# A graph attention layer on one core: the second layer of two steps' radial MLP as four 64x64 quadrants, and transfers spread over the steps

## The chip, the cores and the metric

The kernel runs on one core of a Trainium2 chip. The time is device time of one execution in microseconds (us); three executions of the kernel before took 6774.2, 6771.05 and 6747.99 us, median 6771.05. PE is the matmul engine (PEld its weight loads), ACT the engine for activations, DVE the vector engine, POOL the engine that issues the gathers, SP the one that issues the other transfers. Everything is float32.

## The reference

There are 12500 nodes and 400000 edges, sorted by destination. Each edge has 32 attributes, a weight, a source and a destination. Cut to what matters:

```
h       = relu(layernorm(x))
message = (h @ w_src + b_src)[src] + (h @ w_dst)[dst]
r       = silu(edge_attr @ w1 + b1)          # 32 -> 64
r       = silu(r @ w2 + b2)                  # 64 -> 64
message = message * edge_weight * (r @ w3 + b3)   # 64 -> 128
message = message @ w_sep + b_sep            # per head: 16 for the score, 16 values
score   = sum(smooth_leaky_relu(a) * alpha_dot)   # 8 heads
att     = softmax of score over the edges of one destination
out     = x + segment_sum(values * att) @ w_proj + b_proj
```

The three products with w1, w2 and w3 are the radial MLP, "first", "second" and "third layer" below.

## The kernel before

Node tables (h @ w_src, h @ w_dst) are made first. Then the edges are worked through in 400 *pairs*, numbered k; a pair is 1000 edges, two sections f = 0, 1 of 500 edges, each section four tiles of 125. At the end partial sums at the sections' ends are combined and projected. Nearly all the time is the loop over k in `passes` (from L882 on). One pass of it, a step, does the message of pair k and the weighted sums of pair c = k - 12, because the softmax needs the scores of whole groups of eight pairs.

The order on each engine is the order in which the program is written, `tc.manual_schedule()`. In step k, before the change:

- SP: the stores of pair c - 1 (win, and half of agg), then loads: every eighth step, at k % 8 = 1, the edge attributes of eight pairs (`load_e`, eight transfers of 125 KB in 128-byte rows, L688), in odd steps the destinations of two pairs (`load_d`, L695), then the weights of pair k + 2 spread over all partitions (`load_w`, 500 KB, L701) and two windows of the destination table (`load_md`, L707), and last the other half of agg (L878).
- POOL: eight gathers of source rows for pair k + 4 (L714). Their buffer gs has four copies, so the gathers of k + 4 start when the transposes of pair k (L766) have read theirs.
- PE, in this order: third layer of pair k (L754); eight transposes of gathered rows into pm (L766) and the destination rows added (L771); values of pair c, first half (L855); alphas(k, 0) (L779); values, second half; first layer of pair k + 2 (L732); second layer of pair k + 1 (L740); alphas(k, 1); sums of pair c (L866); the transposes of the attributes of pair k + 3 (`e_T`, L724); in odd steps scores (L790).
- ACT: the SiLU passes after alphas (sl, L781), first layer (h, L735) and second layer (h, L742), copies of the sums (ob, L870) and of the transposed attributes (eT, L726).
- DVE: rad = (third layer + b3) * weight (L757), mT = pm * rad (L775), pvx = values * attention (L857), al (L783) and one-hot matrices.

A product result lies in one of eight banks. Before the change these are: m1 (one bank: e_T and the second layer), p3 (two: first and third layer), pm (two), pa, misc (sums, scores, softmax transposes) and V, one each. A product that writes a bank waits until the last result there has been read. In the profile, names lose their numbers: p stands for p1 and p3, m for m1, h for h1 and h2.

The first layer packs two sections' attributes by 32 and 64 rows, so its result holds f = 0 in partitions 0 to 63 and f = 1 in 64 to 127. The second layer before is one product with a block matrix that has w2 twice on its diagonal (L740). The third layer is two products with 64 rows, one for each section (L754).

Buffers named below: `sp` and `lp` tiles have two copies unless `bufs=` says otherwise; w_b and md have three.

Of the kernel before, what the change touches and what calls it, by code (L numbers as in the profile page):

```python
# [21 lines left out]
F32 = mybir.dt.float32  # L22
BF16 = mybir.dt.bfloat16
I32 = mybir.dt.int32
AF = mybir.ActivationFunctionType
# [5 lines left out]
P = 128  # L31
C = 128
H = 8
RAD = 32
BANK = 512
FC = 64
# [9 lines left out]
T = 125  # L46
TS = 4
SEC = T * TS
W = 64
PR = 2 * SEC  # L50
# [3 lines left out]
EP = 8  # L54
# [3 lines left out]
def gnn_kernel(ctx: ExitStack, tc: tile.TileContext, a: dict, out: bass.AP):  # L58
    nc = tc.nc
# [39 lines left out]
    def load(name, shape, ap=None, eng=None):  # L99
# [14 lines left out]
    part = const.tile([P, 1], F32, name="part")  # L114
    nc.gpsimd.iota(part, pattern=[[0, 1]], base=0, channel_multiplier=1,
                   allow_small_or_imprecise_dtypes=True)
    zc = 5
    assert N % RP == 0 and N // RP % zc == 0
    z = const.tile([RP, zc * ROW], F32, name="z")
    nc.gpsimd.memset(z, 0.0)  # L120
# [482 lines left out]
    def windows():  # L603
        with tc.tile_pool(name="wk", bufs=1) as kp:
            w1b = kp.tile([P, P], F32, name="w1b")
            nc.vector.memset(w1b, 0.0)
            w2b = kp.tile([P, P], F32, name="w2b")
            nc.vector.memset(w2b, 0.0)
            w3b = kp.tile([P, C], F32, name="w3b")
            b12 = kp.tile([P, 2], F32, name="b12")  # L610
            for f in range(2):
                for q in range(2):
                    r = (2 * q + f) * RAD
                    nc.sync.dma_start(out=w1b[r:r + RAD, f * FC:(f + 1) * FC], in_=a["fc_w1"])
                s = slice(f * FC, (f + 1) * FC)
                nc.sync.dma_start(out=w2b[s, s], in_=a["fc_w2"])
                nc.sync.dma_start(out=w3b[s, :], in_=a["fc_w3"])
                nc.sync.dma_start(out=b12[s, 0:1], in_=a["fc_b1"])
                nc.sync.dma_start(out=b12[s, 1:2], in_=a["fc_b2"])
            w_s = kp.tile([C, 32], F32, name="w_s")  # L620
            nc.vector.memset(w_s, 0.0)
            nc.vector.tensor_copy(w_s[:, 0:H], w_score[:, 0:C:C // H])
            b_s = kp.tile([P, 1], F32, name="b_s")
            tgt = kp.tile([P, NP], F32, name="tgt")
            with tc.tile_pool(name="tg", bufs=1) as gp, tc.tile_pool(name="tg_ps", bufs=1, space=PSUM) as gq:
                pb = gq.tile([P, 1], F32, name="pb")
                for j in range(4):
                    nc.tensor.matmul(pb[32 * j:32 * j + 32, :], w_s, b_a, start=True, stop=True)
                nc.vector.tensor_scalar(b_s, pb, 0.25, None, op0=ALU.mult)
                tb = gp.tile([P, NP], I32, name="tb")  # L630
                nc.sync.dma_start(out=tb[0:W, :], in_=base_d[0:1, :].to_broadcast([W, NP]))
                nc.sync.dma_start(out=tb[W:P, :], in_=base_d[1:2, :].to_broadcast([W, NP]))
                row = gp.tile([P, 1], F32, name="row")
                nc.vector.tensor_copy(row, part)
                nc.vector.tensor_scalar(row[W:P, :], part[W:P, :], float(W), None, op0=ALU.subtract)
                nc.vector.tensor_scalar(tgt, tb, row, None, op0=ALU.add)
            passes(kp, w1b, w2b, w3b, b12, w_s, b_s, tgt)
        combine()

    def passes(kp, w1b, w2b, w3b, b12, w_s, b_s, tgt):  # L640
        src_t = src.rearrange("(t p) -> t p", p=T)
        dst_t = dst.rearrange("(t p) -> t p", p=T)
        ea_t = ea.rearrange("(t p) c -> p t c", p=T)
        dst_p = dst.rearrange("(k f e) -> f k e", f=2, e=SEC)
        ew_p = ew.rearrange("(k e) o -> o k e", e=PR)
        with tc.tile_pool(name="ld", bufs=2) as lp, tc.tile_pool(name="wk2", bufs=2) as sp, \
# [33 lines left out]
                nc.vector.tensor_copy(loc, pt[:, 1, :])  # L680
                prep[u] = (idx, loc)

            def load_e(g):
                e_g[g] = lp.tile([T, EP * 8, RAD], F32, name="e_t")
                for f in range(2):
                    for t in range(TS):
                        o = t % 2 * 4 + t // 2 * 2 + f
                        nc.sync.dma_start(  # L688
                            out=e_g[g][:, o::8, :],
                            in_=ea_t[:, g * 8 * EP + f * TS + t:(g + 1) * 8 * EP:8, :])  # L690

            def load_d(g):
                d_g[g] = lp.tile([P, 2, SEC], I32, name="d_b")
# [3 lines left out]
                        in_=dst_p[f:f + 1, 2 * g:2 * g + 2, :].to_broadcast([W, 2, SEC]))  # L697

            def load_w(k):
                w_g[k] = lp.tile([P, PR], F32, name="w_b", bufs=3)  # L700
                nc.sync.dma_start(out=w_g[k], in_=ew_p[:, k, :].to_broadcast([P, PR]))  # L701

            def load_md(k):
                md[k] = lp.tile([P, C], F32, name="md", bufs=3)
                at = [nc.sync.value_load(base[0:1, f, k:k + 1]) for f in range(2)]
                for f in range(2):
                    nc.sync.dma_start(out=md[k][f * W:(f + 1) * W, :], in_=t_dst[ds(at[f], W), :])  # L707
# [20 lines left out]
            def mlp1(k):  # L728
                p1 = pp.tile([P, 2, BANK], F32, name="p3")
                for q in range(2):  # L730
                    s = slice(q * 2 * RAD, (q + 1) * 2 * RAD)
                    nc.tensor.matmul(p1[:, q, 0:2 * T], w1b[s, :], eTs[k][s, :],  # L732
                                     start=True, stop=True)
                h1s[k] = sp.tile([P, SEC], F32, name="h1")
                nc.scalar.activation(h1s[k].rearrange("p (q e) -> p q e", q=2), p1[:, :, 0:2 * T],  # L735
                                     AF.Silu, bias=b12[:, 0:1], scale=1.0)

            def mlp2(k):
                p2 = pp.tile([P, SEC], F32, name="m1")
                nc.tensor.matmul(p2, w2b, h1s.pop(k), start=True, stop=True)  # L740
                h2s[k] = sp.tile([P, SEC], F32, name="h2")
                nc.scalar.activation(h2s[k], p2, AF.Silu, bias=b12[:, 1:2], scale=1.0)  # L742


            def one_hot_T(k):
# [3 lines left out]

            def mlp3(k):  # L750
                p3 = pp.tile([C, 2, BANK], F32, name="p3")
                for f in range(2):
                    s = slice(f * FC, (f + 1) * FC)
                    nc.tensor.matmul(p3[:, f, 0:SEC], w3b[s, :], h2s[k][s, :], start=True, stop=True)  # L754
                rads = [sp.tile([C, SEC], F32, name="rad", bufs=3) for _ in range(2)]
                for f in range(2):
                    nc.vector.scalar_tensor_tensor(rads[f], p3[:, f, 0:SEC], b3, w_g[k][:, f * SEC:(f + 1) * SEC],  # L757
                                                   op0=ALU.add, op1=ALU.mult)
                return rads
# [120 lines left out]
            def has(k):  # L880
                return 0 <= k < NP

            prep_load(0)
            prep_make(0)
            load_e(0)
            for k in range(-5, NP + LAG + 2):
                c = k - LAG
                if has(c - 1):
                    store_win(c - 1)
                    store(c - 1, 0)  # L890

                if k % 16 == 4 and has(k + 12):
                    prep_load((k + 12) // 16)
                if k % EP == 1 and has(k + EP + 3):
                    load_e((k + EP + 3) // EP)
                if k % 2 and has(k + 3):
                    load_d((k + 3) // 2)
                if has(k + 2):
                    load_w(k + 2)
                    load_md(k + 2)  # L900
                if has(k + 4) and (k + 4) % MP == 0:
                    load_sm((k + 4) // MP)
                if has(c - 1):
                    store(c - 1, 1)
                if 0 <= 2 * k < NZ:
                    for i in range(2 * k, min(2 * k + 2, NZ)):
                        zero(i)
                if k % 16 == 8 and has(k + 8):
                    prep_make((k + 8) // 16)
                if has(k + 4):  # L910
                    gather(k + 4)
                if has(c):
                    sums_begin(c)
                if has(k):
                    message(k, mlp3(k))
                if has(c):
                    values(c, 0)
                if has(k):
                    alphas(k, 0)
                if has(c):  # L920
                    values(c, 1)
                if has(k + 2):
                    mlp1(k + 2)
                if has(k + 1):
                    mlp2(k + 1)
                    one_hot_T(k + 1)
                if has(k):
                    alphas(k, 1)
                if has(c):
                    sums(c)  # L930
                m, r = divmod(k, MP)
                if has(k - MP):
                    if r == 1:
                        softmax_up(m - 1)
                    elif r == 2:
                        softmax_down(m - 1)
                        softmax_exp(m - 1)
                    elif r == 3:
                        softmax_T(m - 1)
                if has(k + 3):  # L940
                    e_T(k + 3)
                if has(k) and k % 2 == 1:
                    scores(k)

# [177 lines left out]
```

## Time and profile before

| what | value |
|---|---|
| median of three executions | 6771.05 us |
| profiled execution | 6912.5 us |
| its span, first to last instruction | 6910.7 us |
| mean granted PE clock | 0.851 of full |
| busy DVE, ACT | 42%, 26% of the span |
| DMA | 113 GB/s in the mean |

The profile is of one execution, 2.1% longer than the median of the others. In the lists of groups a line gives code line, engine, operation, tiles (out<-in), shapes, count, then busy us and mean ns of one, then the idle us of the engine before it and what ended them. A matmul of float32 values is recorded as two instructions for each product. A line of waits gives engine and tile, what it waited for, total us, how often, and the longest. A line of the timeline gives start, length, engine, line, operation, and in brackets the idle time before it and what ended it. A line of windows gives a stretch, its length, busy us and number of PE, PEld, DVE, ACT, POOL, then granted clock, DMA share and GB/s. A wait on several events is put down to the one that came last by the profile, which need not be the true one; "remote" and "issue" name none.

### The profile page before, as it was taken

The numbers are of one execution on the slowest core, as the hardware profiler recorded it, in microseconds if no ns is written. First come the engines' busy times: TensorE is split into PE (matmuls) and PEld (weight loads), VectorE is DVE, ScalarE is ACT, GpSimd is POOL, SyncE is SP. The second block draws the span as 40 slices with busy tenths as digits, with TensorE's granted clock in tenths as the row PEclk, the third lists the DMA queues.
The fourth block names the chain that finished last, engine by engine and source line by source line (L and its number), as shares of the span: only waits on it lengthen the run. The fifth ranks groups of instructions, "written<-read, shape, count | busy, mean of one in ns | idle before, by whom it ended". The sixth has DMA issues, their size and how long they took to land. (4 is left out here: it accounts for less than half of the span.)

```text
span 6910.7 us, 80466 instructions
## 1 busy us (share of the span) xinstructions
PE 5257.1 (76%) x26512; PEld 2738.3 (40%) x26512; DVE 2906.8 (42%) x5422; ACT 1792.4 (26%) x3905; POOL 3108.4 (45%) x3234
## 2 busy tenths in 40 slices
PE   4577787787787777777777787877777778787846
PEld 3234444344444333444444444434444434443433
DVE  4244344344344343444444444444444444443447
ACT  3122222222222222222222222222222222222211
POOL 0454454454444444444444444444444444454420
PEclk7788888888888888888888888888888888888975
DMA  3454444444444444454444454444444544444414
GB/s 118 141 139 110 114 118 115 107 117 119 108 115 116 106 111 113 114 119 112 109 118 111 113 122 113 117 118 114 117 114 108 119 113 109 119 116 107 115 39 110
DMA packets 933810, 783.10 MB, mean 113 GB/s; under 512 B 541327, under 2 KB 824918, under 8 KB 933133
## 3 DMA queue, kind: packets, MB, share of 16 engines
q1 hardware_dynamic: 813668, 560.00, 30.3%
q0 software_dynamic: 103552, 210.81, 13.9%
q10 hardware_dynamic: 16162, 7.06, 0.4%
q8 instruction: 212, 3.47, 0.2%
q14 instruction: 216, 1.76, 0.1%
HBM read 643.13 MB, written 134.70 MB: 113 GB/s over the span
## 5 line engine op out<-in xcount | busy, mean ns | idle before, releaser
L714 POOL DMA_INDIRECT gs<-t_src,idx x3200 | 3069.7, 959 | 3467.6 <-PE pm L766 2123.2
L783 DVE SCALAR_TENSOR_TENSOR al<-pa,sl 128x500 f32<-128x500 f32 x800 | 542.6, 678 | 2172.6 <-ACT sl L781 1546.6
L781 ACT ACTIVATE sl<-pa,c_b_a 128x500 f32<-128x500 f32 x800 | 541.4, 677 | 2032.1 <-PE V L855 739.3
L855 PEld LDWEIGHTS V<-c_w_v,mT 128*125 128x125 f32 x6400 | 770.2, 189 | 665.7 <-issue 366.3
L757 DVE SCALAR_TENSOR_TENSOR rad<-p,c_fc_b,w_b 128x500 f32<-128x500 f32 x800 | 552.8, 732 | 998.3 <-PE p L754 867.9
L779 PE MATMUL pa<-mT,c_w_a 128*128 128x500 f32 x1600 | 836.4, 605 | 165.4 <-DVE mT L775 137.0
L855 PE MATMUL V<-c_w_v,mT 128*125 128x128 f32 x6400 | 921.4, 287 | 30.5 <-DVE pvx L857 9.9
L790 PE MATMUL misc<-al,w_s 128*32 128x500 f32 x1600 | 374.4, 971 | 470.3 <-ACT ob L870 449.5
L754 PE MATMUL p<-h,w3b 64*128 64x500 f32 x1600 | 656.6, 910 | 0.0
L775 DVE TENSOR_TENSOR mT<-pm,rad 128x500 f32<-128x500 f32 x800 | 504.1, 671 | 323.2 <-PE pm L771 291.7
L766 PEld LDWEIGHTS pm<-ident,gs 125*128 125x128 f32 x3200 | 456.5, 177 | 459.6 <-issue 458.1
L857 DVE TENSOR_TENSOR pvx<-V,Pem 125x512 f32<-125x512 f32 x800 | 545.4, 682 | 190.0 <-PE m L740 49.2
L766 PE MATMUL pm<-ident,gs 125*128 125x125 f32 x3200 | 565.4, 335 | 0.0
L735 ACT ACTIVATE h<-p,b 128x500 f32<-128x500 f32 x400 | 270.8, 677 | 1124.9 <-PE pa L779 255.1
L724 PE MATMUL m<-ident,e_t 125*128 125x125 f32 x800 | 195.1, 331 | 478.0 <-ACT h L742 312.5
L771 PE MATMUL pm<-ohT,md 64*128 64x500 f32 x1600 | 520.8, 686 | 14.5 <-issue 7.4
L866 PE MATMUL misc<-pvx,oh 125*64 125x136 f32 x6400 | 484.7, 287 | 43.4 <-DVE pvx L857 29.8
L866 PEld LDWEIGHTS misc<-pvx,oh 125*64 125x64 f32 x6400 | 371.0, 137 | 342.0 <-issue 313.1
L740 PE MATMUL m<-h,w2b 128*128 128x500 f32 x800 | 450.4, 645 | 0.0
L779 PEld LDWEIGHTS pa<-mT,c_w_a 128*128 128x128 f32 x1600 | 272.7, 193 | 399.1 <-issue 188.2
L742 ACT ACTIVATE h<-m,b 128x500 f32<-128x500 f32 x400 | 270.5, 676 | 361.6 <-PE misc L866 99.1
L724 PEld LDWEIGHTS m<-ident,e_t 125*128 125x128 f32 x800 | 95.3, 157 | 570.4 <-ACT h L742 360.1
(137 smaller groups left out, 3225.6 us busy)
## 6 DMA issues: line engine op xcount, KB each, us to landing
w_b<-in_edge_weight SPq DMA_DIRECT2D x400, 500.0 KB
d_b<-in_dst SPq DMA_DIRECT2D x400, 250.0 KB
gs<-t_src,idx POOLq DMA_INDIRECT x3200
e_t<-in_edge_attr SPq DMA_DIRECT2D x400, 125.0 KB
sc_d<-Sp SPq DMA_DIRECT2D x200, 250.0 KB
win<-ob SPq DMA_DIRECT2D x400, 68.0 KB
agg<-ob SPq DMA_DIRECT2D x800, 34.0 KB
md<-t_dst SPq DMA_DIRECT2D x800, 32.0 KB
```

The lines of the kernel that those rows point to most:

```text
L714: nc.gpsimd.indirect_dma_start(out=gs[:, j, :], out_offset=None, in_=t_src[:, :], in_offset=bass.IndirectOffsetOnAxis(ap=idx[:, t:t + 1], ...
L754: nc.tensor.matmul(p3[:, f, 0:SEC], w3b[s, :], h2s[k][s, :], start=True, stop=True)
L757: nc.vector.scalar_tensor_tensor(rads[f], p3[:, f, 0:SEC], b3, w_g[k][:, f * SEC:(f + 1) * SEC], op0=ALU.add, op1=ALU.mult)
L766: nc.tensor.matmul(pm[f][:, t * T:(t + 1) * T], gs[:T, f * TS + t, :], ident[:T, :T], start=(t == 0), stop=False, is_transpose=True, skip_ ...
L771: nc.tensor.matmul(pm[f], md[k][s, :], ohT[k][s, :], start=False, stop=True, skip_group_check=True)
L775: nc.vector.tensor_mul(mTs[k][:, f * SEC:(f + 1) * SEC], pm[f], rads[f])
L779: nc.tensor.matmul(pa, w_a, mTs[k][:, f * SEC:(f + 1) * SEC], start=True, stop=True)
L781: nc.scalar.activation(sl, pa, AF.Silu, bias=b_a, scale=1.0)
L783: nc.vector.scalar_tensor_tensor(al, pa, 0.25, sl, op0=ALU.mult, op1=ALU.add)
L855: nc.tensor.matmul(V[:, t, :], mTs[c][:, o:o + T], w_v, start=True, stop=True)
L857: nc.vector.tensor_mul(pvx[c][:, f, :, 0:C].rearrange("p t (h k) -> p t h k", h=H), V.rearrange("p t (h k) -> p t h k", h=H), Pem[c // MP] ...
L866: nc.tensor.matmul(acc[f * W:(f + 1) * W, :], ohs[c][:, f * TS + t, :], pvx[c][:, f, t, :], start=(t == 0), stop=(t == TS - 1), skip_group ...
```

## The change

The second layer is done for two pairs at once, in steps with even k: for each of the pairs k + 1 and k + 2 and each section, one 64x64 product. The pair j = 0 keeps its sections at their halves of the partitions, the pair j = 1 crosses them, so that the four products lie in the four quadrants of the array. Their results go to two banks of p3 and are read by one ACT pass of 1000 columns. The matrix w2b now holds w2 in all four quadrants. The third layer takes its rows from the half where its section lies.

The first layer is done for pair k + 3 instead of k + 2, and ahead of alphas(k, 0) instead of behind the second values; h1 has three copies. The transposes of the attributes go one pair further ahead as well. The weights and windows are loaded three steps ahead, four copies each, ahead of load_d. The eight attribute transfers of a group are issued one a step (two in the first) over seven steps, behind these loads. The zeros that agg is filled with at the start go in 25 pieces instead of 20.

```diff
-    zc = 5
+    zc = 4
...
             w2b = kp.tile([P, P], F32, name="w2b")
-            nc.vector.memset(w2b, 0.0)
...
-                nc.sync.dma_start(out=w2b[s, s], in_=a["fc_w2"])
+                for q in range(2):
+                    nc.sync.dma_start(out=w2b[s, q * FC:(q + 1) * FC], in_=a["fc_w2"])
...
-            def load_e(g):
-                e_g[g] = lp.tile([T, EP * 8, RAD], F32, name="e_t")
-                for f in range(2):
-                    for t in range(TS):
-                        o = t % 2 * 4 + t // 2 * 2 + f
-                        nc.sync.dma_start(
-                            out=e_g[g][:, o::8, :],
-                            in_=ea_t[:, g * 8 * EP + f * TS + t:(g + 1) * 8 * EP:8, :])
+            def load_e(g, i):
+                if i == 0:
+                    e_g[g] = lp.tile([T, EP * 8, RAD], F32, name="e_t")
+                f, t = divmod(i, TS)
+                o = t % 2 * 4 + t // 2 * 2 + f
+                nc.sync.dma_start(out=e_g[g][:, o::8, :],
+                                  in_=ea_t[:, g * 8 * EP + i:(g + 1) * 8 * EP:8, :])
...
-                w_g[k] = lp.tile([P, PR], F32, name="w_b", bufs=3)
+                w_g[k] = lp.tile([P, PR], F32, name="w_b", bufs=4)
...
-                md[k] = lp.tile([P, C], F32, name="md", bufs=3)
+                md[k] = lp.tile([P, C], F32, name="md", bufs=4)
...
-                h1s[k] = sp.tile([P, SEC], F32, name="h1")
+                h1s[k] = sp.tile([P, SEC], F32, name="h1", bufs=3)
...
             def mlp2(k):
-                p2 = pp.tile([P, SEC], F32, name="m1")
-                nc.tensor.matmul(p2, w2b, h1s.pop(k), start=True, stop=True)
-                h2s[k] = sp.tile([P, SEC], F32, name="h2")
-                nc.scalar.activation(h2s[k], p2, AF.Silu, bias=b12[:, 1:2], scale=1.0)
+
+                p2 = pp.tile([P, 2, BANK], F32, name="p3")
+                h2 = sp.tile([P, 2, SEC], F32, name="h2")
+                js = [j for j in range(2) if has(k + j)]
+                for j in js:
+                    for f in range(2):
+                        s = slice(f * FC, (f + 1) * FC)
+                        o = slice((f ^ j) * FC, ((f ^ j) + 1) * FC)
+                        nc.tensor.matmul(p2[o, j, 0:SEC], w2b[s, o], h1s[k + j][s, :], start=True, stop=True)
+                    h2s[k + j] = (h2, j)
+                t = slice(js[0], js[-1] + 1)
+                nc.scalar.activation(h2[:, t, :], p2[:, t, 0:SEC], AF.Silu, bias=b12[:, 1:2], scale=1.0)
...
             def mlp3(k):
                 p3 = pp.tile([C, 2, BANK], F32, name="p3")
+                h2, j = h2s.pop(k)
                 for f in range(2):
-                    s = slice(f * FC, (f + 1) * FC)
-                    nc.tensor.matmul(p3[:, f, 0:SEC], w3b[s, :], h2s[k][s, :], start=True, stop=True)
+                    s = slice((f ^ j) * FC, ((f ^ j) + 1) * FC)
+                    nc.tensor.matmul(p3[:, f, 0:SEC], w3b[s, :], h2[s, j, :], start=True, stop=True)
...
-                if k % EP == 1 and has(k + EP + 3):
-                    load_e((k + EP + 3) // EP)
+                if has(k + 3):
+                    load_w(k + 3)
+                    load_md(k + 3)
                 if k % 2 and has(k + 3):
                     load_d((k + 3) // 2)
-                if has(k + 2):
-                    load_w(k + 2)
-                    load_md(k + 2)
+                g, r = divmod(k + 4, EP)
+                if k >= -4 and r < EP - 1 and has((g + 1) * EP):
+                    for i in ((0, 1) if r == 0 else (r + 1,)):
+                        load_e(g + 1, i)
...
                 if has(c):
                     values(c, 0)
+                if has(k + 3):
+                    mlp1(k + 3)
                 if has(k):
                     alphas(k, 0)
                 if has(c):
                     values(c, 1)
-                if has(k + 2):
-                    mlp1(k + 2)
+                if k % 2 == 0 and (has(k + 1) or has(k + 2)):
+                    mlp2(k + 1)
                 if has(k + 1):
-                    mlp2(k + 1)
                     one_hot_T(k + 1)
...
-                if has(k + 3):
-                    e_T(k + 3)
+                if has(k + 4):
+                    e_T(k + 4)
```

More of the change, by code (lines that the diff above doesn't have):

```diff
@@ L884, in passes @@
             prep_make(0)
-            load_e(0)
+            for i in range(8):
+                load_e(0, i)
             for k in range(-5, NP + LAG + 2):
```

## The prediction

> **What bounds the kernel now.** A step is one pass of the loop over k; a step with odd k ends in scores. I read the page first (which engine is full), then the waits (who waits in bulk), then one stretch of the timeline (in which order), then the loop's last steps, where one engine is missing.
>
> ```profile
> PE 5257.1 (76%) x26512; PEld 2738.3 (40%) x26512; DVE 2906.8 (42%) x5422; ACT 1792.4 (26%) x3905; POOL 3108.4 (45%) x3234
> L714 POOL DMA_INDIRECT gs<-t_src,idx x3200 | 3069.7, 959 | 3467.6 <-PE pm L766 2123.2
> L754 PE MATMUL p<-h,w3b 64*128 64x500 f32 x1600 | 656.6, 910 | 0.0
> L740 PE MATMUL m<-h,w2b 128*128 128x500 f32 x800 | 450.4, 645 | 0.0
> ```
>
> No engine is full. PE leads with 76%, but that is busy time in part at half clock. Now the waits:
>
> ```profile
> POOL gs L714 <- PE pm L766: 2123.2, 288, 12.2
> PE misc L790 <- ACT ob L870: 449.5, 136, 4.5
> PE m L724 <- ACT h L742: 312.5, 156, 5.3
> PE pa L779 <- DVE mT L775: 137.0, 112, 15.9
> ```
>
> The gathers wait for the transposes L766, which free their buffer; PE waits for the copy ob, and for the second layer's ACT pass. No transfer stands among the large waits. The order, from an odd step into an even one:
>
> ```profile
> 3005.85 0.69 PE L732 MATMUL p<-eT,w1b 64*128 64x250 f32 x4
> 3006.47 1.11 PE L740 MATMUL m<-h,w2b 128*128 128x500 f32 x2
> 3006.59 0.68 ACT L735 ACTIVATE h<-p,b 128x500 f32<-128x500 f32 x1 [1.17 <-PE p L732]
> 3008.28 0.68 ACT L742 ACTIVATE h<-m,b 128x500 f32<-128x500 f32 x1 [1.01 <-PE m L740]
> 3008.35 1.15 PE L866 MATMUL misc<-pvx,oh 125*64 125x136 f32 x16
> ...
> 3010.73 0.94 POOL L714 DMA_INDIRECT gs<-t_src,idx  x1 [0.30 <-issue]
> ...
> 3013.63 0.27 ACT L870 COPY ob<-misc 128x136 f32<-128x136 f32 x1 [2.40 <-remote]
> ...
> 3013.96 1.89 PE L790 MATMUL misc<-al,w_s 128*32 128x500 f32 x8 [4.10 <-ACT ob L870]
> ...
> 3015.78 2.04 PE L754 MATMUL p<-h,w3b 64*128 64x500 f32 x4
> ...
> 3017.75 1.39 PE L766 MATMUL pm<-ident,gs 125*128 125x125 f32 x8
> ...
> 3019.41 0.94 POOL L714 DMA_INDIRECT gs<-t_src,idx  x1 [7.74 <-PE pm L766]
> ```
>
> The sums (L866) end at 3009.50, but ACT copies them only at 3013.63, 4.1 us later, with nothing else in front of it. That is 1.96 us after the last gather (3011.67). The same without gathers, in the loop's last steps:
>
> ```profile
> 6565.52 1.15 PE L866 MATMUL misc<-pvx,oh 125*64 125x136 f32 x16
> 6566.74 0.27 ACT L870 COPY ob<-misc 128x136 f32<-128x136 f32 x1 [0.44 <-PE misc L866]
> ...
> 3001.80:3019.40 17.60, 13.08 (x67) 6.43 (x68) 7.25 (x12) 4.35 (x11) 7.70 (x8) 0.81 0.42 120
> 6566.70:6577.10 10.40, 9.99 (x64) 5.34 (x66) 6.22 (x11) 3.20 (x7) 0.00 (x0) 1.00 0.12 40
> ```
>
> There the copy follows at 0.07 us, and a step takes 10.4 us. So while POOL gathers, PE's completions reach the other engines late: those from about 4 us after the first gather are held, come out a few at a time, and the rest about 2 us after the last gather. Listing each step's first gather and the first following start of each line gives the loop's law. An even step's floor is 12.2 us (eight gathers 9.7, 1.9 until the completions come, 0.6 to restart); its mean is 13.5, and 89 of 200 exceed 12.6; the excess over the floor is 253 us in all. An odd step averages 18.1: after the hold come ob, scores, third layer and transposes, mostly at half clock, and only then the next gather. The two make up 6312 us of the 6911.
>
> **The skill.** "TensorE: Matmul & The Clock Gate", Part 1, says that a 3.4 us window of idle PE halves its clock. The trace agrees: after the 4.10 us stall, third-layer matmuls take 2.04 us instead of 1.11, and that step's mean clock is 0.81. Its Part 3 (packing) says that tiles at different row and column positions run at once. The trace shows it by halves only: L754's two 64-row products take 1.11 us together, as one 128-row product in L740 does, and four 32-column products of L790 take 1.04 at full clock; the 64x64 grid is not shown. "SBUF — State Buffer", Who interferes with whom, says of the SBUF's ports that PE and ACT wait for nobody; here PE's completions do stand behind POOL's gathers, 4.1 us against 0.07, by whatever path, and the measurement decides.
>
> **The change, part by part.**
> Second layer. Every step now spends one product of 1.04 us start to start; then four quadrants, about 1.04 if they overlap, on even steps only. PE saves 0.52 us a step, 208 us over 400. On odd steps this is PE work ahead of the 4.1 us stall: the stall grows by what is saved. On even steps the product stays. So its face value is not gained.
> Its eviction. ACT takes 0.374 us for 250 columns and 0.677 for 500, 1.21 ns a column, so 1000 columns take about 1.28 us against 2 x 0.68.
> First layer. The product of 0.62 us moves before alphas(k,0), from 3.8 to about 1.8 us after the first gather, before the hold. Its ACT pass then follows at once instead of at a median of 7.2 (even) or 5.8 us (odd). On PE it fills the wait for mT (137 us) where there is one; elsewhere alphas(k,0) and the second value product end 0.6 us later, the latter at 4.45 instead of 3.83 us, at the edge of the hold.
> Banks. e_T no longer shares m1 with the second layer, so its 312 us of waiting goes. But the second layer now shares p3, so the third layer of k+1 waits for the whole 1.28 us pass. What is late next is the third layer instead of e_T. Where held completions come together, old: h1 0.68, h2 0.68, e_T 0.36, third layer, 1.72 us; new: 1.28 + 0.05. That is 0.4 us earlier, worth something only in the 89 late even steps: 89 x 0.4 = -36 us.
> Odd steps. ACT has neither first nor second layer left before ob when the hold ends. ob now starts 11.5 us after the first gather in the best steps and 11.9 median, 12.0 mean; I take 0.3 x 200 = -60 us.
> Transfers. Eight e_t pieces held SP 14.8 us in one step of eight. Now it issues one more piece (two once) in seven of eight steps, at about 0.5 us free and 2.0[...], ahead of load_sm and the second agg store, behind w_b, md and d_b. SP's stores free ob, three buffers deep, so 2 us there is covered by more than a step; without that cover it would cost those 2 us in a step. The wait for the e_t buffer falls when SP has already waited for ob. Nothing large waits for w_b or md, so the third step of prefetch gains nothing. One thing is lost: the steps with k%8 = 1, when e_t kept the large loads out of the gathers, are the shortest odd ones (17.3 us against 17.9 at k%8 = 5). 50 x 0.5 = +25 us. zc, the dropped memset and two more weight loads touch only the prologue: nothing.
> Sum: -36 - 60 + 25 = -71 us on the profiled 6912.5 us (span 6910.7 and 1.8 around it); the median 6771.05 is 0.98 of that, so -70: **6701 us**.
>
> **Unknown costs.** Quadrants: between 1.04 us (all four overlap) and 2.1 (two at a time); I take 1.04, since both directions overlap in the trace. Held completions: between 0.6 us a late step gained, if fewer are queued, and 1.0 lost, if the value product joins them; I take it as unchanged in number. Half clock: no gain and up to 1 us in a late even step.
>
> **The rivals.**
> 1. Small gain as summed: 6701, own range 6630 to 6735. For it: e_T's wait and ACT's queue before ob. Against it: the hold ends with POOL, whatever PE does. 0.42.
> 2. Large gain: with the first layer out of the hold, late even steps vanish: 253 + 60 - 25 = 288, times 0.98: 6489. For it: late steps begin with a late h1. Against it: another product takes its place in the queue. 0.12.
> 3. Nothing: all falls into the stall and the gathers' time: 6771. 0.14.
> 4. Slower: the second value product is now the first one held. The sums wait for its DVE pass, e_T and the third layer stand behind the sums on PE. From the release: 0.68 + 1.08 + 0.36 = 2.12 us instead of 1.72; and where PE then idles a clock window, the sums run at half clock too, 1.08 more in about half of the cases. 89 x (0.4 + 0.54) + 25 = 109, times 0.98: 6878. For it: 4.45 us is just where the first layer's product ended (4.47) and was held. It decides once the sums start, at the median of even steps, later than about 8.8 us after the first gather instead of 6.28. 0.27.
> 5. The quadrants do not overlap: the pass comes 1.04 us later in the 89 steps, 92 us, less what case 1 gains in odd steps and plus the 25: 57, times 0.98: 6827. 0.05.
>
> **How the numbers follow.** Within 0.5% (34 us) is what a measurement of this kernel can't tell from no change. Faster 0.42 + 0.12 = 0.54, same 0.14, slower 0.27 + 0.05 = 0.32. The range 6530 to 6885 takes in cases 1, 3, 5, most of 4 and the upper part of 2.
>
> **What would show it.** h1 (ACT) within 4 us of the first gather; no wait of e_T for h; L740's successor at about 1.04 us for four quadrants in even steps only; ob at 11.5 to 11.7 us in odd steps; even steps' mean below 13.4. Wrong, if the sums wait for pvx in bulk, if even steps grow longer, or if the hold no longer ends with POOL.

## The result and the profile after

The changed kernel is slower: 7079.8 us, median of four executions (6991.67 to 7125.84), against 6768.94 us for the kernel before (6747.99 to 6774.2). The ratio is 1.0424, with a 95% interval of 1.037 to 1.0477. It is taken over fast runs alone, without the longest of the four (7125.84 us), and so is not the quotient of the two medians. The profiled execution took 6991.67 us, with a span of 6989.9 us and a mean PE clock of 0.839.

One thing has to be said first, since the numbers below can't be read without it. The late completions that the prediction reads off the profile (a result of PE that the next engine takes up only microseconds after PE's end) belong to some *sessions* (runs made together on one chip), not to the kernel. In four sessions the kernel before took 6752 to 6910 us and completions came late. In five it took 5225 to 5231 us and they did not. Whether this belongs to a chip, to its machine or to the hour is not known; chip number 11 stands in one session of each kind, but whether that is one and the same chip is not known. The first comparison, of both kernels, is of the late kind.

From the page of the changed kernel, engines and groups in the columns of before:

```profile
PE 5149.3 (74%) x27312; PEld 2720.0 (39%) x27312; DVE 2921.5 (42%) x5421; ACT 1737.3 (25%) x3706; POOL 3125.7 (45%) x3234
L713 POOL DMA_INDIRECT gs<-t_src,idx x3200 | 3087.0, 965 | 3530.1 <-PE pm L774 2338.3
L762 PE MATMUL p<-h,w3b 64*128 64x500 f32 x1600 | 676.3, 936 | 442.8 <-ACT h L749 338.7
L749 ACT ACTIVATE h<-p,b 128x1000 f32<-128x1000 f32 (+1 forms) x201 | 219.2, 1090 | 1031.6 <-remote 567.6
```

PE has 108 us less to do (5257.1 before), and the kernel is still longer. The third layer (L762), which waited for nobody before (0.0), now stands idle for 442.8 us, most of it for the joint second-layer pass (L749). ACT stands idle 1031.6 us ahead of that pass. From the list of waits of the changed kernel:

```profile
POOL gs L713 <- PE pm L774: 2338.3, 344, 12.6
ACT h L749 <- remote: 567.6, 81, 7.9
PE misc L798 <- ACT ob L878: 501.3, 137, 5.5
PE p L762 <- ACT h L749: 338.7, 132, 5.2
PE misc L874 <- DVE pvx L865: 100.9, 75, 5.7
```

The wait of e_T for the second layer (312.5 us) is gone, as forecast. A wait of the third layer took its place, and the gathers wait 215 us more for the transposes behind it. The sums wait for pvx only 100.9 us. The timeline shows one long even step (the lines of PE, ACT and the gathers at its ends):

```profile
3057.39 0.95 POOL L713 DMA_INDIRECT gs<-t_src,idx  x1 [7.04 <-PE pm L774]
...
3059.90 0.68 ACT L734 ACTIVATE h<-p,b 128x500 f32<-128x500 f32 x1 [4.39 <-PE V L863]
3060.72 1.04 PE L863 MATMUL V<-c_w_v,mT 128*125 128x128 f32 x8
...
3061.69 1.07 PE L746 MATMUL p<-h,w2b 64*64 64x500 f32 x8
...
3063.56 0.69 DVE L865 TENSOR_TENSOR pvx<-V,Pem 125x512 f32<-125x512 f32 x1 [1.25 <-PE p L746]
3063.72 1.73 PE L874 MATMUL misc<-pvx,oh 125*64 125x136 f32 x16
...
3066.15 0.95 POOL L713 DMA_INDIRECT gs<-t_src,idx  x1 [0.31 <-issue]
3069.41 1.09 ACT L749 ACTIVATE h<-p,b 128x1000 f32<-128x1000 f32 x1 [7.81 <-remote]
...
3070.56 2.04 PE L762 MATMUL p<-h,w3b 64*128 64x500 f32 x4 [4.75 <-ACT h L749]
...
3072.52 1.93 PE L774 MATMUL pm<-ident,gs 125*128 125x125 f32 x8
...
3074.73 0.95 POOL L713 DMA_INDIRECT gs<-t_src,idx  x1 [7.63 <-PE pm L774]
```

The quadrants overlap (1.07 us for all four) and end at 3062.76. ACT, idle, starts their pass only at 3069.41, 6.65 us later and 2.31 us after the last gather's end. Then third layer and transposes run at half clock (2.04 and 1.93 us, at a granted clock of 0.50). This long even step, and beside it a stretch of about one short even step, in the view of windows:

```profile
3057.30:3074.60 17.30, 12.42 (x68) 6.67 (x68) 6.72 (x11) 3.68 (x8) 7.57 (x8) 0.85 0.40 109
2997.70:3010.10 12.40, 11.96 (x75) 6.36 (x73) 5.33 (x9) 3.13 (x5) 7.64 (x8) 1.00 0.49 126
```

Most even steps are now of two kinds, about 12.1 us (the short one here at full clock) or about 16.8 (the long one at 0.85).

### The profile page after: what moved, and what is told of

Same layout as the page of the kernel before. It is cut to its first block, busy times and chain, and to the rows that moved or that the text cites. A ratio compares the mean times of both kernels' runs of the same rounds, so it can differ in the third digit from the quotient of the medians.

```text
span 6989.9 us, 82125 instructions
## 1 busy us (share of the span) xinstructions
PE 5149.3 (74%) x27312; PEld 2720.0 (39%) x27312; DVE 2921.5 (42%) x5421; ACT 1737.3 (25%) x3706; POOL 3125.7 (45%) x3234
## 5 line engine op out<-in xcount | busy, mean ns | idle before, releaser
L787 PE MATMUL pa<-mT,c_w_a 128*128 128x500 f32 x1600 | 890.5, 639 | 155.7 <-issue 93.2
L762 PE MATMUL p<-h,w3b 64*128 64x500 f32 x1600 | 676.3, 936 | 442.8 <-ACT h L749 338.7
L863 PE MATMUL V<-c_w_v,mT 128*125 128x128 f32 x6400 | 880.8, 281 | 10.1 <-DVE pvx L865 9.9
L874 PE MATMUL misc<-pvx,oh 125*64 125x136 f32 x6400 | 562.0, 299 | 199.7 <-DVE pvx L865 100.9
L874 PEld LDWEIGHTS misc<-pvx,oh 125*64 125x64 f32 x6400 | 418.1, 143 | 522.9 <-issue 412.8
L749 ACT ACTIVATE h<-p,b 128x1000 f32<-128x1000 f32 (+1 forms) x201 | 219.2, 1090 | 1031.6 <-remote 567.6
L762 PEld LDWEIGHTS p<-h,w3b 64*128 64x128 f32 x1600 | 172.2, 263 | 767.0 <-issue 385.9
L787 PEld LDWEIGHTS pa<-mT,c_w_a 128*128 128x128 f32 x1600 | 239.2, 188 | 486.2 <-issue 284.9
L731 PE MATMUL p<-eT,w1b 64*128 64x250 f32 x1600 | 277.9, 423 | 76.6 <-DVE rad L765 39.3
L878 ACT COPY ob<-misc 128x136 f32<-128x136 f32 x400 | 109.0, 272 | 894.2 <-remote 603.7
```

Source lines behind the costliest of these rows:

```text
L762: nc.tensor.matmul(p3[:, f, 0:SEC], w3b[s, :], h2[s, j, :], start=True, stop=True)
L787: nc.tensor.matmul(pa, w_a, mTs[k][:, f * SEC:(f + 1) * SEC], start=True, stop=True)
L863: nc.tensor.matmul(V[:, t, :], mTs[c][:, o:o + T], w_v, start=True, stop=True)
L874: nc.tensor.matmul(acc[f * W:(f + 1) * W, :], ohs[c][:, f * TS + t, :], pvx[c][:, f, t, :], start=(t == 0), stop=(t == TS - 1), skip_group ...
```

## The experiments

The steps are counted from first gather to first gather, 174 even and 174 odd ones in the middle of the loop. A is the theory that the joint second layer is what comes late, B that the spread transfers lengthen the late time, and A2, formed later, that the place of the second layer is to blame.

| kernel | session | of before, interval | even, odd us | even steps over 15 us |
|---|---|---|---|---|
| before (e5) | late | 6778 us | 12.99, 18.31 | 21 |
| transfers alone (e7) | late | 0.9964 [0.9942, 0.9985] | 12.84, 18.10 | 19 |
| changed (e6) | late | 1.0431 [1.037, 1.0492] | 14.63, 18.07 | 91 |
| both early (e8) | late | 1.0788 [1.0722, 1.0855] | 15.66, 17.97 | 106 |
| unpaired (e16) | late | 0.9922 [0.9898, 0.9946] | 12.91, 18.23 | 18 |
| first layer earliest, banks (e15) | late | 0.9867 [0.9808, 0.9926] | 16.71, 14.66 | 164 |
| transfers alone (e1) | without | 0.9511 [0.9495, 0.9526] | 10.12, 11.85 | 0 |
| products alone (e2) | without | 0.9851 [0.9835, 0.9868] | 10.16, 12.87 | 0 |
| changed (e13) | without | 0.9369 [0.9352, 0.9386] | 10.16, 11.43 | 0 |
| unpaired (e9) | without | 0.9259 [0.924, 0.9277] | 10.61, 10.65 | 0 |
| first layer in odd steps (e10) | without | 0.9253 [0.923, 0.9275] | 10.42, 10.87 | 0 |
| transfers, banks (e11) | without | 0.9399 [0.938, 0.9418] | 10.12, 11.51 | 0 |
| changed, banks (e12) | without | 0.9261 [0.9242, 0.9279] | 10.18, 11.09 | 0 |
| two passes (e17) | without | 1.0036 [1.0023, 1.0048] | 11.97, 11.43 | 0 |
| full products (e18) | without | 0.9535 [0.9519, 0.955] | 10.64, 11.43 | 0 |

### The two halves, and no gathers (e1 to e4)

e1 is before with the change's transfers (`load_e` in pieces, `load_w` and `load_md` three steps ahead, four buffers, zc 4). e2 is the changed kernel with the old ones. e3 and e4 are before and changed without the gathers: one buffer of 0.5 stands in for every gathered row.

```diff
-                gs = lp.tile([P, 8, C], F32, name="gs", bufs=4)
...
-                    nc.gpsimd.indirect_dma_start(
...
-                gath[k] = gs
+                gath[k] = gs_one
```

> The kernel before with the change's transfers alone: the eight attribute pieces spread over seven steps, weights and windows three steps ahead with four copies, ahead of the destinations, 25 zero pieces; the products as before. Theory A (the joint second layer's completion is held until the gathers end, and the third layer behind it): the transfers cost nothing, 6740 to 6810 us. Theory B (the spread transfers keep traffic in every step's gathers and so lengthen the hold): most of the 311 us, 6950 us or more.

> The changed kernel with the transfers of the kernel before: attributes in one burst of eight, weights and windows two steps ahead with three copies. Theory A: slow as the changed kernel, 7000 to 7120 us. Theory B: 6700 to 6800 us.

> The kernel before without its gathers: one tile set to a constant once stands for the gathered rows of all pairs, so the output is not the reference's. If the hold comes from the gathers (both theories), steps take 10.1 to 10.5 us as in the last steps of the loop, 6769 - 400 x 5.5 = about 4550 us (4400 to 4800). If the late completions have another cause, above 6000 us.

> The changed kernel without its gathers, as in the run without gathers of the kernel before. Theories A and B: with no hold PE is the bound, and the 0.52 us of PE work saved in a step are gained, 150 to 210 us below the kernel before without gathers. Theory C (the joint pass of 1000 columns and the shared banks p3 cost time by themselves, hold or no hold): no gain or a loss against it.

Every absolute number was missed, since before took 5225.88 us there (5219.8 to 5237.74). Against it: e1 4970.91 us, e2 5149.6, e3 4972.73 (0.9514) and e4 4874.4 (0.9325). e4 is 98 us below e3, where 150 to 210 were expected.

ob follows the sums by 0.05 us (median) in e1 and e2 *with* the gathers running; in the profile of before it was 4.25. So gathers alone don't make completions late. e1, with the new transfers, and e3, with the old ones but no gathers, end within 2 us of each other; no run joins before's products, the new transfers and no gathers. What the transfers gain in such a session is seen in the waits for DMA of e2, which still has the burst of eight:

```profile
PE pm L780 <- DMA md<-t_dst: 189.7, 50, 21.2
DVE rad L766 <- DMA w_b<-in_edge_weight: 155.3, 51, 19.9
```

Some 50 times, once in eight steps, the windows and weights come late behind the burst; a step with k % 8 = 3 then takes 18.0 us in e2, in e13 12.3. In e13, with the transfers spread, neither wait is among the large ones. In e3, with before's products, the burst is there and the gathers are not, and the same two waits are only 46.4 and 41.5 us. This suggests that most of the burst's cost arises where it meets the gathers.

### Is it the chip, and is it the transfers (e5 to e8)

e5 and e6 are the two kernels themselves, e7 is e1 again, and e8 moves the first layer ahead of the first values and the joint second layer directly behind them:

```diff
+                if has(k + 3):
+                    mlp1(k + 3)
                 if has(c):
                     values(c, 0)
-                if has(k + 3):
-                    mlp1(k + 3)
+                if k % 2 == 0 and (has(k + 1) or has(k + 2)):
+                    mlp2(k + 1)
                 if has(k):
                     alphas(k, 0)
                 if has(c):
                     values(c, 1)
-                if k % 2 == 0 and (has(k + 1) or has(k + 2)):
-                    mlp2(k + 1)
```

> The kernel before, for its profile on the chip of these runs. Theory H (the late completions belong to the chip, not to the kernel): either about 5226 us with the copy ob 0.05 us behind the sums although the gathers run, or about 6770 us with 4.2 us behind them, nothing in between. Rival (the late completions come from the kernel's own order, and the earlier 5226 us was a chip that is faster in everything): a lag of about 4 us here whatever the time.

> The changed kernel. Theory H, on a chip without late completions: as the two parts and the kernels without gathers say, about 0.933 of before (4875 us), since there the transfers alone gave 0.951, the products alone 0.985 and the changed kernel without gathers 0.9325. On a chip with late completions: 1.03 to 1.05 of before, as the first measurement. Rival (the change loses by itself, 1.04, whatever the chip): 1.04 on both.

> Before with the transfers of the change alone. On a chip with late completions: theory A (the joint second layer's completion is what they hold) 0.99 to 1.01, theory B (the spread transfers lengthen the hold) 1.03 or more. On a chip without them both give 0.951 again.

> The changed kernel with the first layer ahead of the first values and the joint second layer directly behind them. On a chip with late completions: theory A expects the joint pass within 5 us of the first gather in nearly all even steps, no even steps of 16 to 17 us, and 0.98 or less of before; theory B no less than 1.03. On a chip without them: within 0.5% of the changed kernel, a little above if the second layer then waits for the first layer's pass.

The session was a late one. e6 repeats the loss (7044.32 us; 1.0431), and all of it lies in the even steps: +1.64 us, times 200 are 328 us, against -0.24 us, or 48, in the odd ones (the profiled run of e5 is 26 us above its session's median, so 0.1 us a step is not clear of noise). e7 shows that the transfers have no part in it (6731.05 us): B falls. e8 failed the expectation of A: the joint pass came early, as asked (median 4.3 us after the first gather, past 10 us in one step of 174), and the kernel still got slower (7263.88 us). One of its long steps shows how:

```profile
3090.32 1.07 PE L746 MATMUL p<-h,w2b 64*64 64x500 f32 x8
...
3091.45 1.10 ACT L749 ACTIVATE h<-p,b 128x1000 f32<-128x1000 f32 x1 [1.42 <-PE p L746]
3092.26 1.04 PE L863 MATMUL V<-c_w_v,mT 128*125 128x128 f32 x8
...
3097.36 0.69 DVE L865 TENSOR_TENSOR pvx<-V,Pem 125x512 f32<-125x512 f32 x1 [3.51 <-remote]
...
3098.11 2.07 PE L874 MATMUL misc<-pvx,oh 125*64 125x136 f32 x14 [2.72 <-DVE pvx L865]
```

Here the second value product ends at 3093.30 and is seen at 3097.36. The sums wait for it, and everything behind them. In 169 of the 174 even steps this product is seen over 1 us late (in e6 in 105). Here, moving one product ahead of the late time pushed another into it.

### The place or the pairing (e9, e10, e14, e15, e16)

In e6 the second value product ends 4.37 us after the first gather, in e5 at 3.85; that suggested A2. e9 and e16 are one kernel: the change with before's second layer, one pair a step in m1, in every step at the change's place.

```diff
-                if k % 2 == 0 and (has(k + 1) or has(k + 2)):
-                    mlp2(k + 1)
                 if has(k + 1):
+                    mlp2(k + 1)
                     one_hot_T(k + 1)
```

> The changed kernel (first layer ahead of alphas(k, 0), new transfers), but the second layer for one pair a step in bank m1, as before. On a chip with late completions: theory A (the joint second layer is what comes too late) 0.98 to 1.01, even steps near 13 us. Theory A2 (the first layer, put ahead, pushes the second value product into the held ones, one more in front of the second layer, paired or not) 1.03 or more. On a chip without them: about 0.95 by either.

> The changed kernel with the second layer for one pair a step in bank m1, as before, its place and all else as in the change. On a chip with late completions: theory A (joint pass is late by itself) even steps of about 13 us, 0.98 to 1.01 of before. Theory A2 (its place behind the held second value product is what counts, paired or not) even steps above 14 us and, as odd steps now need a second layer too, 1.03 to 1.06. On a chip without them: 0.926 again.

In the late session e16 took 6827.92 us, 0.9922 of before, with even steps of 12.91 us. Its second value product still ends at 4.37 us and is seen over 0.5 us late in 166 steps of 174 (in e6 in 110; without late completions, in e9 and e13, it is 0.47). So the place is not it, and A2 falls. With the pairing undone the loss is gone: second-layer passes past 10 us stand in 15 even steps of 174, in e6 in 93. Nor does the joint product end later: the medians are 5.37 us after the first gather in e6, 5.21 in e16 and 5.51 in e5. The waits of the gathers and for the second layer's pass, e6 and then e16:

```profile
POOL gs L713 <- PE pm L774: 2386.8, 342, 12.4
PE p L762 <- ACT h L749: 362.6, 133, 5.2
...
POOL gs L713 <- PE pm L765: 1954.1, 272, 13.5
PE m L723 <- ACT h L741: 87.0, 114, 14.6
```

e6 and e16 are of two sessions, in which before itself differs by 2% (6752.18 and 6885.11 us); each is compared with its own. A step of e16 with the same start of PE's work as the long one above:

```profile
3070.64 1.04 PE L854 MATMUL V<-c_w_v,mT 128*125 128x128 f32 x8
...
3071.51 1.00 PE L739 MATMUL m<-h,w2b 128*128 128x500 f32 x2
...
3073.86 0.69 DVE L856 TENSOR_TENSOR pvx<-V,Pem 125x512 f32<-125x512 f32 x1 [1.63 <-PE pa L778]
...
3074.59 0.68 ACT L741 ACTIVATE h<-m,b 128x500 f32<-128x500 f32 x1 [3.07 <-PE pa L778]
...
3076.11 1.11 PE L753 MATMUL p<-h,w3b 64*128 64x500 f32 x4
```

The one pair's product ends at 3072.51 and its pass starts 2.1 us later, on the heels of pvx; the third layer runs at full clock (1.11 us). In the changed kernel's step the pass came 5.85 us after pvx, here 0.73. These are single steps; the counts above say how often each kind occurs.

e10 and e14 (one kernel) put the first layer of two pairs in the odd steps and the joint second layer alone in the even ones; both came to sessions without late completions and so say nothing on A2:

```diff
-                if has(k + 3):
+                if k % 2 and has(k + 3):
                     mlp1(k + 3)
                 if has(k):
                     alphas(k, 0)
+                if k % 2 and has(k + 4):
+                    mlp1(k + 4)
...
-                if has(k + 4):
-                    e_T(k + 4)
+                if has(k + 5):
+                    e_T(k + 5)
```

> The changed kernel with the first layer of both pairs in the odd steps, so that in even steps the second values end before the hold again and the joint second layer is the first one held. On a chip with late completions: theory A2 even steps of 12.2 to 13 us, 0.96 to 0.99 of before; theory A (joint is late by itself) even steps above 14 us, 1.03 or more. On a chip without them: within 1% of the changed kernel.

> The changed kernel with the first layer of both pairs in the odd steps, on a chip with late completions if these runs get one: theory A2 (the first layer, put ahead, pushes the second value product into the held completions, in front of the second layer) even steps of 12.2 to 13 us, 0.96 to 0.99 of before; theory A (the joint second layer is late by itself) even steps above 14 us, 1.03 or more. On a chip without them 0.925 again.

Measured: 4838.33 us for e10 and, in the next session, 4835.07 us (0.924 [0.922, 0.926]) for e14.

### Two banks moved (e11, e12, e15)

In late sessions an odd step of before is 5 us longer than an even one, in large part because scores wait for ob's bank. e11 (on the transfers alone) and e12 (on the changed kernel) give scores alphas' bank and the softmax transposes the values' bank. e15 adds to e12 the first layer ahead of the first values.

```diff
-                ps = pp.tile([P, SEC], F32, name="misc")
+                ps = pp.tile([P, SEC], F32, name="pa")
...
-                pt = pp.tile([T, TS, P], F32, name="misc")
+                pt = pp.tile([T, TS, P], F32, name="V")
```

> Before with the transfers of the change, scores in the bank of alphas (pa) instead of that of the sums, softmax transposes in the bank of the values. On a chip with late completions the odd steps need not wait for the copy ob any more: odd steps of 12.5 to 14 us instead of 18.1, together 0.83 to 0.88 of before. If instead the third layer or alphas' own passes end last in odd steps, they stay above 16 us and it is 0.95 or more. On a chip without them: 0.94 to 0.955, as the transfers alone.

> The changed kernel with the same two banks moved. On a chip with late completions: theory A and A2 both leave even steps at 14.6 us, odd ones 12.5 to 14, 0.87 to 0.93 of before and so above the kernel with the transfers and banks alone. On a chip without them: about 0.93, or what the changed kernel gives there.

> The changed kernel with the first layer one place further ahead (before the first values, where PE waits for mT anyway), and scores in alphas' bank, softmax transposes in the values' bank. On a chip with late completions: theory A2 expects the second value product of even steps to end at about 4.1 instead of 4.37 us after the first gather, its DVE pass within 0.5 us of that in most steps instead of 39%, even steps of 12.3 to 13.2 us instead of 14.6; theory A (joint is late by itself) even steps above 14 us as before. Odd steps, by the banks alone, 12.5 to 15 us instead of 18.1. Together A2 0.80 to 0.87, A 0.87 to 0.92. On a chip without late completions: 0.92 to 0.93, as the changed kernel with the banks alone.

e11 took 4913.64 us and e12 4838.83. Only e15 met a late session: 6800.96 us. Odd steps fell from 18.1 (e6, another session) to 14.66 us. That is the banks' doing, since e8 has the first layer in the same place without them, and its odd steps stayed at 17.97. But even steps rose to 16.71, and the ratio, 0.9867, is above what either theory expected: in 165 of 174 the joint pass starts past 10 us. From its waits:

```profile
ACT h L749 <- remote: 1100.7, 150, 8.4
...
PE p L762 <- ACT h L749: 566.4, 165, 5.5
```

The same two waits as in the changed kernel, at 1.9 and 1.7 times the size that they have in the first profile. The second value product ended at 4.2 to 4.7 us, not at the 4.1 expected, so e15 is no test of A2.

### The change without late completions, and which part of the pair (e13, e17, e18)

> The changed kernel once more. On a chip without late completions (before about 5225 us): theory H says 0.92 to 0.935, as its parts and its two variants there; the rival (it loses by itself) 1.04. On a chip with them (before about 6760): 1.04 again, for comparison with the next run.

e13, the changed kernel, took 4899.73 us: 0.9369 of before. There the change is a gain of 6%. Its timeline:

```profile
3017.11 1.07 PE L746 MATMUL p<-h,w2b 64*64 64x500 f32 x8
...
3018.25 1.09 ACT L749 ACTIVATE h<-p,b 128x1000 f32<-128x1000 f32 x1 [1.23 <-PE p L746]
...
3019.14 1.15 PE L874 MATMUL misc<-pvx,oh 125*64 125x136 f32 x16
...
3020.34 0.27 ACT L878 COPY ob<-misc 128x136 f32<-128x136 f32 x1 [0.41 <-PE misc L874]
...
3020.59 1.11 PE L762 MATMUL p<-h,w3b 64*128 64x500 f32 x4
```

The pass follows the quadrants by 0.07 us and ob the sums by 0.05, beside running gathers. Even steps last 10.16 us.

e17 reads the quadrants by two passes, and e18 replaces them by two products with the block matrix under one pass:

```diff
-                t = slice(js[0], js[-1] + 1)
-                nc.scalar.activation(h2[:, t, :], p2[:, t, 0:SEC], AF.Silu, bias=b12[:, 1:2], scale=1.0)
+                    nc.scalar.activation(h2[:, j, :], p2[:, j, 0:SEC], AF.Silu, bias=b12[:, 1:2], scale=1.0)
```

```diff
-                        nc.tensor.matmul(p2[o, j, 0:SEC], w2b[s, o], h1s[k + j][s, :], start=True, stop=True)
+                    nc.tensor.matmul(p2[:, j, 0:SEC], w2b, h1s[k + j], start=True, stop=True)
```

> The changed kernel, its four quadrants in the same place, but read by two ACT passes of 500 columns, one for each pair behind its own two products, instead of one of 1000. In a session with late completions: if the one pass over both pairs is what comes late (theory A, pass), the first pass sees its completion as early as the unpaired one, even steps near 13 us and 0.97 to 1.00 of before; if the quadrants themselves or the banks p3 are (theory A, products), even steps above 14 us and 1.03 or more. In a session without them: the second pass starts 0.7 us after the first, 0.93 to 0.945 of before, as the changed kernel's 0.937.

> The changed kernel with the joint second layer made of two products with the block matrix (128 rows, 128 columns) instead of four quadrants; one ACT pass over both pairs and the banks p3 as in the change. In a session with late completions: if the pass over both pairs or its banks come late, even steps above 14 us and 1.03 or more of before; if the quadrants do, 13 to 13.5 us and 1.01 or less. In a session without them: the second layer takes 2.1 us instead of 1.07 in even steps, which PE lacks there: even steps 0.9 to 1.1 us longer than the changed kernel's 10.16, so 0.975 of before against its 0.937.

Neither met a late session, so which part of the pair comes late stays open. e17 took 5248.51 us, far from the 0.93 to 0.945 expected: the second pair's products waited for the first pass on the shared tile, as its timeline shows.

```profile
3017.79 1.06 PE L746 MATMUL p<-h,w2b 64*64 64x500 f32 x4
...
3018.89 0.68 ACT L748 ACTIVATE h<-p,b 128x500 f32<-128x500 f32 x1 [1.19 <-PE p L746]
...
3019.62 1.05 PE L746 MATMUL p<-h,w2b 64*64 64x500 f32 x4 [0.78 <-ACT h L748]
```

Two quadrants alone take 1.06 us, as long as all four together. The second two, with the wait of 0.78 us ahead of them, make 1.84 us, and even steps are 1.81 us longer than in e13. e18 took 4988.04 us. In a step of its trace the second layer takes 1.84 us of PE against 1.07; its even steps grow by 0.48 us (10.64 against 10.16), 0.9 to 1.1 being expected, so only a part of what the quadrants save on PE reaches the step.

## Why the prediction was wrong

**The step that failed** is the one under "Banks": "Where held completions come together, old: h1 0.68, h2 0.68, e_T 0.36, third layer, 1.72 us; new: 1.28 + 0.05. That is 0.4 us earlier", with the assumption under "Unknown costs" that held completions are "unchanged in number". It compares the work after a release and takes the release itself as the same. It is not: even steps in which the second-layer pass starts past 10 us went from 22 to 93 of 174 (e5, e6). In e6 these take 16.63 us, the others 12.33, so each costs about 4.3 us, partly at half clock. By the prediction's own measure, even steps over 12.6 us, they went from 47 to 112 of 200; its 89 belonged to one long execution. So the term is not -36 but, with all else that changed in even steps, about +328 us.

e16 shows the cause as far as it is settled: the joint second layer, by quadrants, pass or banks, and not its place; e7 clears the transfers. Why the joint pass misses its release more often stays open. The misses are not spread evenly either: in e6, 71 of the 93 fall in steps with k % 4 = 0 and 22 in those with k % 4 = 2, of which there are 87 each, and no run says why.

The price bounds given, "1.0 lost" a late step and up to 1 us for the clock, together 2 us, were too small, because they priced one more product in the queue and not a miss of the moment of release.

**The late completions as a law of POOL's gathers.** This came from one profile and a loop tail that lacked gathers *and* loads. In e13 the gathers run and nothing is late. It can hold in late sessions only, and there too the gathers' part is a reading, since no run without gathers met one. The text had no case for the other sessions, where the change gains 6%.

**Quadrants and their pass.** Right: 1.07 us against 1.04, 1.09 us against 1.28. Rival 5 is out.

**e_T's wait gone, the third layer late next.** Right in kind. It was sized as 0.05 us behind the pass; it is 338.7 us of waiting.

**Odd steps, -60 us.** Near in size (-0.24 us a step against -0.3), but the mechanism is not shown. e7 has both layers on ACT ahead of ob, as before, and its odd steps are 18.10 us, so the transfers alone give 0.21 of the 0.24. The prediction had put the transfers at a loss there; that the size fits is luck.

**PE's 208 us not gained.** Right in late sessions. Elsewhere e18 puts the quadrants' share at 88 us, across two sessions (4988.04 against 4899.73 in e13).

**Transfers +25 us, third step of prefetch nothing.** The sign was wrong, the size small: e7 gives 0.9964, or -24 us. Without late completions the same edit gains 4.9%, as the burst then stands on the path (e2's waits). In the profile of before no such wait is large; that its long steps hid the burst is the likely reading, not tested.

**Rival 4** had the right sign for another reason. The second value product is indeed held (over 0.5 us in 106 even steps of the profile after), but the sums start at 6.3 us, far from the 8.8 where it was to decide, and e16 has even more such holds without the loss. Its mechanism shows only in e8, where the sums start at a median of 8.1 us.

## What to carry to other kernels

Before a stall is taken as a rule of the kernel, repeat the kernel before in another session: here the largest stall of the profile was absent in five of nine, and the change gained 6% there and lost 4% elsewhere. Where completions come late, count how often a release is missed and not only the work behind it: with two second layers joined, 93 of 174 even steps missed it, with one 15 to 22. Whether one wait for two results does this, or the quadrants or the banks, was not separated. Run a change also without its boldest part: here the change with its second layer unpaired is ahead of both kernels in both kinds of session (0.9922 and 0.9259 of before).

## What the runs showed of the hardware

Late completions are there in some sessions and not in others, with the kernel before 29% longer (6752 against 5226 us); what sets them is not known. In the late profiles the recorded PE completions (updates of the semaphore through which PE tells the others) come out in clusters in even steps, at about 4.4, 5.7, 7.1, 8.5, 9.9 and 11.5 us after a step's first gather; the gathers' packets end in clusters at about 4.5, 5.7, 6.9, 8.3, 9.5 and 10.7. Between 4 and 11 us an even step has 2.65 of them before, 2.08 after the change, 1.18 in e15, and 16 in e13. That the landing gathers let them out is a reading of these times, not shown by an experiment.
